# Inverse square roots of both layer norms: eleven operations on two engines, or one power operation on GpSimd

## The chip, the cores and the metric

The kernel runs on one core of a Trainium2 chip. The metric is the device time of one execution in microseconds (us), the median over runs of the same program. The core has a matrix engine (TensorE, PE in the profile, with PEld for its weight loads), a vector engine (VectorE, DVE), an activation engine (ScalarE, ACT), GpSimd (POOL) and a queue for transfers (SyncE, SP). [...]

## The reference, cut to what matters

Two layers of the same kind run one after the other on an image `x` of 512 x 512 positions with 64 channels, in float32. Both first normalise over groups of two channels of the whole image (`_gn`). Then, for each position:

```python
xn = _ln(x, norm_scale, norm_bias)                      # inner norm over 64 channels
left = (xn @ Wl + bl) * mask * sigmoid(xn @ Wlg + blg)  # 128 hidden channels
right = (xn @ Wr + br) * mask * sigmoid(xn @ Wrg + brg)
out_gate = sigmoid(xn @ Wog + bog)
out = _banded_ingoing(left, right, 4)     # 9 neighbouring rows, weighted by left
out = _ln(out, out_norm_scale, out_norm_bias) * out_gate   # outer norm over 128
return out @ Wo + bo                                    # added to x by the caller
```

and `_ln` is `(x - m) / sqrt(v + eps) * scale + bias`. So every position needs two inverse square roots, one for the inner norm and one for the outer norm, and every layer needs 32 more for its groups.

## The kernel before, in words

The rows are cut into 9 overlapping blocks of 64 and the columns into chunks of 128 positions per half. The work goes in steps: one step (a "unit") brings 8 columns of both halves into the machine, 128 partitions x 512 values, called `z`. There are 288 units per layer, and the stages of one unit are spread over some 30 steps, so that in one step each engine works on several units of different ages.

What an engine does in one step, and in which order, is written out by hand: the lists `FIRST` and `SECOND` (lines 36 to 55) name the stages for the first and the second layer. The loop at line 872 walks the list and emits each stage's instructions, and every engine keeps that program order (`InOrder`, line 383). Therefore nearly every row of the profile carries line 391. The groups have to be told apart by the tiles that they write and read.

GpSimd does most of the elementwise work on `z`: it scales (`z<-z,ga`) and moves it (`z<-z,gb`) for the group norm, centres it (`z<-z,sti`) and rescales it (`z<-z,rs`) for the inner norm, and adds a bias to the rows that come back in (`XR<-XR,fewer` or `both`). VectorE does the statistics (`sti`, `sto`), the product with the sigmoid (`RO<-banks,sg`), and the copies of the banded product back into `RO`.

In every fourth step `solve` (line 623) collects 32 inner and 32 outer variances of each partition into one tile `var` of 128 x 64 and takes their inverse roots into `rs`. The stages are these:

- "solve on a": ScalarE writes the inner half of `var` and the negated outer means `nm`.
- "solve on p": GpSimd writes the outer half of `var` in two operations.
- "solve on d": VectorE writes a first guess into `rs`, one operation on the bits of `var` taken as integers.
- "roots": GpSimd improves that guess in ten operations on 128 x 64 (`rsqrt`, lines 173 to 182), then multiplies the outer part by the mask and `nm` by the result. The items `("roots", 2)` and `("roots", 99)` emit two, or all remaining, of these.

`rs` and `nm` are then read by GpSimd (`z<-z,rs`, "rescale") and by ScalarE (`on<-RO,nm,rs`, "norm") in later steps. Between "solve on p" and "roots" GpSimd has one large operation on `z` in both lists; among the roots it has none.

The same function `rsqrt` serves `group_affine` (line 325), once per layer, ahead of its first unit; there all eleven operations are on VectorE, and their result `ga` is needed by the first `z<-z,ga`.

Of the kernel before, what the change touches and what calls it, by code (L numbers as in the profile page):

```python
# [8 lines left out]
F32 = mybir.dt.float32  # L9
I32 = mybir.dt.int32  # L10
AF = mybir.ActivationFunctionType
ALU = mybir.AluOpType
# [4 lines left out]
P = 128  # L17
# [11 lines left out]
NB = 32  # L29
# [8 lines left out]
    ("out stats", 3), ("project", 4), "turn", "centre", ("sigmoid", 0), "move",  # L38
    "scale next", ("out stats", 99), "solve", "bias", ("solve on", "p"), ("right", 0),
    "last product", "rescale", ("solve on", "a"), ("sigmoid", 4), ("norm", (0, 4)),  # L40
    ("solve on", "d"), "transpose", ("roots", 2), ("right", 4), ("band", 0), "keep",
    ("copy a", 0), ("band", 1), ("roots", 2), "sums", ("copy a", 1), ("roots", 2),
    "norm columns", ("roots", 2), ("roots", 99), "times gate", "move next", ("copy b", 0),
    ("copy b", 1), ("norm", (4, 8)), "end",
# [2 lines left out]
    ("out stats", 2), "gates", "centre", ("out stats", 3), ("project", 0), ("project", 4),  # L47
    ("sigmoid", 0), "scale", "rescale", "gated", ("out stats", 99), "inner stats",
    ("right", 0), "solve", "turn", "scale next", "last product", ("solve on", "p"),
    ("solve on", "a"), ("solve on", "d"), "transpose", ("sigmoid", 4), "move", ("roots", 2),  # L50
    "times gate", "end", ("roots", 2), ("band", 0), ("norm", (0, 4)), "norm columns",
    ("roots", 2), ("roots", 2), "keep", ("right", 4), ("copy a", 0), ("band", 1),
    ("roots", 99), ("norm", (4, 8)), ("copy b", 0), "move next", ("copy a", 1),
# [51 lines left out]
def tile_two_banded_layers(  # L105
# [6 lines left out]
    nc = tc.nc  # L112
# [7 lines left out]
    const = ctx.enter_context(tc.tile_pool(name="const", bufs=1))  # L120
    sm = ctx.enter_context(tc.tile_pool(name="sm", bufs=2))
# [30 lines left out]
        same.rearrange("p (g t) -> p g t", t=2), last(pair, 2), 1.0 / (2.0 * L * L), None, ALU.mult  # L152
    )

    def one_bank():
        return ps.tile([P, 512], F32, tag="ps", name="bank")

    def two_banks():
        return ps2.tile([P, 1024], F32, tag="ps2", name="banks")

    def rsqrt(o: bass.AP, v: bass.AP, vec=nc.vector, e=nc.vector) -> list:


        p, n = v.shape
        t, u = (
            sm.tile([P, 3 * NB], F32, tag=f"rsqrt{i}", name="rsqrt", bufs=1)[:p, :n]
            for i in range(2)
        )
        return [
            lambda: vec.tensor_scalar(  # L170
                o.bitcast(I32), v.bitcast(I32), -0.5, float(0x5F3759DF), ALU.mult, ALU.add
            ),
            lambda: e.tensor_tensor(t, o, o, ALU.mult),
            lambda: e.tensor_tensor(t, t, v, ALU.mult),
            lambda: e.tensor_scalar(u, t, -10.0 / 3.0, None, ALU.add),
            lambda: e.tensor_tensor(t, t, u, ALU.mult),
            lambda: e.tensor_scalar(t, t, 5.0, None, ALU.add),
            lambda: e.tensor_tensor(o, o, t, ALU.mult),
            lambda: e.tensor_tensor(t, o, o, ALU.mult),
            lambda: e.tensor_tensor(t, t, v, ALU.mult),  # L180
            lambda: e.tensor_scalar(t, t, -27.0 / 1024.0, 0.5625, ALU.mult, ALU.add),
            lambda: e.tensor_tensor(o, o, t, ALU.mult),
        ]

    PARTS = (
        ("right", 2 * H), ("left", 2 * H), ("gate", H), ("Wo", D), ("ob", 1),
# [60 lines left out]
    def solve_layer(i: int, f: dict, r: dict, tmp, half: bass.AP):  # L247
# [9 lines left out]
        for nm, lo, hi in (("right", 0, 2), ("left", 2, 4), ("gate", 4, 5)):  # L257
            lo, hi = lo * H, hi * H
            pm = one_bank()[:, : hi - lo]
            nc.tensor.matmul(pm, lhsT=half, rhs=aug[:, lo:hi], start=True, stop=True)  # L260
            pb = one_bank()[:, : hi - lo]
            nc.tensor.matmul(pb, lhsT=hb, rhs=raw[:, lo:hi], start=True, stop=False)
            nc.tensor.matmul(pb, lhsT=ones_row, rhs=brow[:, lo:hi], start=False, stop=True)
            nc.vector.tensor_tensor(r[nm], aug[:, lo:hi], pm, ALU.subtract)
            nc.vector.tensor_tensor(r[nm], r[nm], pb, ALU.add)
# [14 lines left out]
        nc.vector.tensor_scalar(r["Wo"], f["wo"], osc, None, ALU.mult)  # L280

        pb = one_bank()
        nc.tensor.matmul(pb[:, :D], lhsT=ones_row, rhs=f["bo"], start=True, stop=True)
        if i == 0:
# [40 lines left out]
    def group_affine(mean: bass.AP, var: bass.AP, pool):  # L325

        ve = pool.tile([P, D], F32, name="g_ve")
        nc.vector.tensor_scalar(ve, var, GN_EPS, None, ALU.add)
        for f in rsqrt(ga, ve):
            f()  # L330
        nc.vector.scalar_tensor_tensor(gb, mean, -1.0, ga, ALU.mult, ALU.mult)
# [291 lines left out]
    def solve(w: dict, ins: list, outs: list, sti, sto) -> dict:  # L623

        ni, no = len(ins) * JU, len(outs) * JU
        v = sm.tile([P, 3 * NB], F32, tag="var", name="var", bufs=1)[:, : ni + no]
        r = sm.tile([P, 3 * NB], F32, tag="rs", name="rs", bufs=3)[:, : ni + no]
        pairs = lambda x: x.rearrange("p (k t) -> p k t", t=2)
        act, pool = [], []
        if ni:  # L630
            of = sti[:, : ni // 2, 2::3]
            act.append(
                lambda: en.scalar.activation(
                    pairs(v[:, :ni]), of, AF.Identity, bias=ln_eps, scale=1.0 / D
                )
            )
            for n, u in enumerate(ins):
                u.rs = r[:, n * JU : (n + 1) * JU]
        if no:

            js = slice(outs[0].m, outs[0].m + no)
            vo = v[:, ni:]
            nm = sm.tile([P, NB], F32, tag="nm", name="nm")[:, :no]
            act.append(lambda: en.scalar.mul(pairs(nm), sto[:, :, 1::3], -1.0))
            pool += [
                lambda: en.gpsimd.tensor_tensor(
                    pairs(vo), sto[:, :, 2::3], pairs(w["m2"][:, js]), ALU.mult
                ),
                lambda: en.gpsimd.tensor_scalar(vo, vo, LN_EPS, None, ALU.add),
            ]  # L650
        seed, *todo = rsqrt(r, v, en.vector, en.gpsimd)
        if no:
            ro = r[:, ni:]
            todo.append(lambda: en.gpsimd.tensor_tensor(ro, ro, w["m"][:, js], ALU.mult))
            todo.append(lambda: en.gpsimd.tensor_tensor(nm, nm, ro, ALU.mult))
            for n, o in enumerate(outs):
                o.rs, o.nm = ro[:, n * JU : (n + 1) * JU], nm[:, n * JU : (n + 1) * JU]
        return {"a": act, "p": pool, "d": [seed], "roots": todo}

    def norm(o: Out, lo: int, hi: int, pool: bool):  # L660
        if lo == 0:
# [107 lines left out]
    def layer(src: bass.AP, dst: bass.AP, w: dict, stats: bool, then=None):  # L769
# [61 lines left out]
        for t in range(min(loads), last_t + 3):  # L831
# [40 lines left out]
            for item in order:  # L872
# [51 lines left out]
                elif name == "end" and p:  # L924
                    ended(dst, p)
                elif name == "sums" and t - 2 in outs:
                    sums(outs[t - 2], t - 2 == first_t, t - 2 == last_t)
                elif name == "solve" and t % 4 == 0:
                    st, us = sti.pop((t + 4) // 4, (None, []))
                    so, os = sto or (None, [])  # L930
                    sto = None
                    if us or os:
                        solving = solve(w, us, os, st, so)
                elif name == "solve on":
                    for f in solving.pop(n, []):
                        f()
                elif name == "roots" and solving:
                    for f in solving["roots"][:n]:
                        f()
                    del solving["roots"][:n]  # L940
                elif name == "norm" and t + 1 in outs:
                    lo, hi = n
                    norm(outs[t + 1], lo, min(hi, JU - nv), False)
                elif name == "norm columns" and t + 1 in outs:
                    norm(outs[t + 1], JU - nv, JU, True)
                elif name == "band" and len(mixing) > n:
                    c, h0 = mixing[n]
                    mixed.append(mix(c, A[c, h0 // HA], h0, stats))
                elif name == "copy a" and len(mixing) > n:
                    en.scalar.copy(*mixed[n][0])  # L950
                elif name == "copy b" and len(mixing) > n:
                    en.vector.tensor_copy(*mixed[n][1])
# [81 lines left out]
    keep = ctx.enter_context(tc.tile_pool(name="keep", bufs=1))  # L1034
# [39 lines left out]
def build(arrays):  # L1074
    import concourse.bacc as _bacc

    nc = _bacc.Bacc("TRN2", target_bir_lowering=False, num_devices=1)
    aps = {}
    for name in _INS:
        a = arrays[f"in_{name}_dram"]  # L1080
        aps[name] = nc.dram_tensor(
            f"in_{name}_dram", a.shape, mybir.dt.from_np(a.dtype), kind="ExternalInput"
        ).ap()
    out = nc.dram_tensor("out_0_dram", aps["x"].shape, F32, kind="ExternalOutput").ap()
    layers = [{n: aps[f"L{i}_conv_{n}"] for n in _NAMES} for i in range(2)]
    with tile.TileContext(nc) as tc:
        tile_two_banded_layers(tc, aps["x"], layers, out)
    return nc
# [10 lines left out]
```

## Time and profile before

| | |
|---|---|
| median of 3 runs | 4811.89 us (4810.83 to 4814.79) |
| the profiled execution's own time | 4837.72 us |
| its span | 4835.9 us |
| busy share of the span | PE 81%, ACT 78%, DVE 77%, POOL 73% |
| granted TensorE clock, mean | 0.942 |

The profiled execution is 25.8 us, or 0.5%, above the median of the runs; 1.8 us of its time lie outside its span. No engine is busy all the time: four of them share the load almost evenly, and the time is set by what they wait for from one another.

Both steady stretches are long: 500 to 2500 us lies within the first layer and 2900 to 4700 us within the second. At 230 and at 2628 us a layer starts, and before 230 us the image is read once for its statistics.

### The profile page before, as it was taken

To read this page: it belongs to the slowest core of one execution; us is meant where nothing else is said; L and a number is where in the kernel's file an instruction comes from. 1 tells how busy PE (TensorE), PEld (TensorE's weight loads), DVE (VectorE), ACT (ScalarE), POOL (GpSimd) and SP (SyncE) were. 2 spreads that over 40 slices of the span, in tenths; PEclk is the share of its full clock that TensorE was granted. 3 is DMA by queue.
4 is the path that set the end of the run, shared out by engine and by line. 5 is a ranking of instruction groups with operands and counts; after the bars stand their busy time and mean duration, and the time that the engine had idled before them with its cause. 6 is when DMAs were issued, how large, how long until landed. Compare 5 with 4: busy or idle time off the path is not lost.

```text
span 4835.9 us, 192971 instructions
## 1 busy us (share of the span) xinstructions
PE 3899.5 (81%) x76306; PEld 3340.4 (69%) x76306; DVE 3737.4 (77%) x9061; ACT 3749.9 (78%) x9022; POOL 3530.7 (73%) x4739
## 2 busy tenths in 40 slices
PE   1035899989998989998985479888888888888898
PEld 0034677777887877887864467777777777777775
DVE  7854777777777777777766468888888888888887
ACT  0023788888888888888886259989888898889899
POOL 0046888888888988998833588878877787777751
PEclk9987999999999999999998689999999999999999
DMA  7968677777777777777764768877777787778776
GB/s 314 393 112 123 175 202 202 203 204 204 199 205 203 208 199 201 207 207 202 199 182 131 72 164 221 223 214 218 216 217 217 211 221 213 218 215 220 218 205 178
DMA packets 1437807, 983.47 MB, mean 203 GB/s; under 512 B 167362, under 2 KB 1284584, under 8 KB 1432552
## 3 DMA queue, kind: packets, MB, share of 16 engines
q1 hardware_dynamic: 1432064, 969.69, 73.7%
q8 instruction: 604, 9.90, 0.9%
q14 instruction: 299, 2.45, 0.2%
q10 hardware_dynamic: 4840, 1.43, 0.1%
HBM read 658.35 MB, written 312.40 MB: 201 GB/s over the span
## 4 chain that ended last, share of the span: by engine, by line
PE 35%; ACT 16%; DMA 11%; POOL 11%; issue 9%; DVE 6%; SPq 4%; POOLq 0%; DVEq 0%; ACTq 0%
PE bank L391 17%; PE banks L391 16%; ACT on L391 9%; POOL z L391 7%; SPq L391 4%; DMA zg<-later 3%; DMA XR<-in_x_dram 3%; ACT gate L391 2%; PE acc L391 2%; ACT zT L391 2%; ACT sg L391 2%; DMA z<-mid_x 2%; POOL rsqrt L391 2%; DVE RO L391 1%; DVE sto L391 1%
## 5 line engine op out<-in xcount | busy, mean ns | idle before, releaser
L391 ACT ACTIVATE on<-RO,nm,rs 128x128 f32<-128x128 f32 x4608 | 1939.9, 509 | 24.5 <-PE bank L391 12.4
L391 PEld LDWEIGHTS banks<-pack,zT 64*128 64x128 f32 x18576 | 1288.9, 203 | 431.7 <-ACT zT L391 250.6
L391 PE MATMUL banks<-pack,zT 64*128 64x128 f32 x18576 | 1321.8, 291 | 213.7 <-ACT zT L391 175.7
L391 DVE TENSOR_TENSOR RO<-banks,sg 128x512 f32<-128x512 f32 (+1 forms) x1188 | 785.0, 674 | 488.5 <-ACT sg L391 367.4
L391 ACT ACTIVATE sg<-banks 128x512 f32<-128x512 f32 (+1 forms) x1188 | 693.3, 598 | 357.6 <-PE banks L391 348.9
L391 POOL TENSOR_TENSOR z<-z,ga 128x512 f32<-128x512 f32 x536 | 682.4, 1282 | 311.9 <-DMA z<-mid_x 214.3
L391 PE MATMUL bank<-zg,pack 64*128 64x448 f32 (+1 forms) x2304 | 684.9, 622 | 194.9 <-DMA zg<-later 123.0
L391 DVE SCALAR_TENSOR_TENSOR ZH<-bank,pack,gate 128x448 f32<-128x448 f32 (+1 forms) x1152 | 739.7, 683 | 95.2 <-ACT gate L391 76.8
L391 DVE BATCH_NORM_STATS2 sto<-RO 128x6 f32<-128x256 f32 x2304 | 799.0, 410 | 2.0 <-ACT RO L391 0.3
L391 POOL TENSOR_TENSOR z<-z,gb 128x512 f32<-128x512 f32 x536 | 681.9, 1281 | 5.0
L391 PE MATMUL bank<-pack,ZH 128*64 128x64 f32 x18432 | 665.7, 225 | 13.1 <-ACT gate L391 11.8
L391 POOL TENSOR_TENSOR z<-z,rs 128x512 f32<-128x512 f32 x586 | 621.2, 1061 | 16.5
L391 PEld LDWEIGHTS bank<-pack,ZH 128*64 128x64 f32 x18432 | 585.9, 138 | 57.3 <-ACT gate L391 22.0
L391 POOL TENSOR_TENSOR z<-z,sti 128x512 f32<-128x512 f32 x586 | 625.1, 1068 | 0.0
L391 ACT ACTIVATE gate<-bank 128x448 f32<-128x448 f32 (+1 forms) x1152 | 568.3, 550 | 49.5 <-PE bank L391 29.0
L391 DVE BATCH_NORM_STATS2 sti<-z 128x6 f32<-128x128 f32 x2344 | 501.7, 280 | 11.6 <-POOL z L391 5.9
L391 ACT ACTIVATE zT<-banks 128x512 f32<-128x512 f32 (+1 forms) x1084 | 470.2, 494 | 30.0 <-PE banks L391 23.5
L391 PE MATMUL bank<-ident,on 64*128 64x64 f32 x9216 | 450.4, 227 | 41.2 <-ACT gate L391 27.2
L391 PEld LDWEIGHTS bank<-ident,on 64*128 64x128 f32 x9216 | 415.4, 141 | 92.4 <-ACT gate L391 37.0
L391 PE MATMUL banks<-RO,A 64*64 64x128 f32 x9216 | 338.0, 289 | 105.9 <-DVE RO L391 99.2
L391 PEld LDWEIGHTS bank<-zg,pack 64*128 64x128 f32 x2304 | 221.6, 193 | 276.5 <-issue 67.3
L391 DVE TENSOR_TENSOR XR<-bank,XR 120x512 f32<-120x512 f32 (+1 forms) x576 | 391.2, 679 | 1.5 <-PE bank L391 0.8
(150 smaller groups left out, 4021.3 us busy)
## 6 DMA issues: line engine op xcount, KB each, us to landing
later<-zT SPq DMA_DIRECT2D x576, 256.0 KB
A<-left_of SPq DMA_DIRECT2D x1152, 128.0 KB
zg<-later SPq DMA_DIRECT2D x576, 256.0 KB
z<-in_x_dram SPq DMA_DIRECT2D x576, 128.0 KB
z<-mid_x SPq DMA_DIRECT2D x576, 128.0 KB
gn_x<-in_x_dram SPq DMA_DIRECT2D x16, 4096.0 KB
XR<-in_x_dram SPq DMA_DIRECT2D x448, 112.0 KB
mid_x<-XR SPq DMA_DIRECT2D x448, 112.0 KB
```

Source lines behind the costliest of these rows:

```text
L391: return lambda *a, **k: tc.keep_in_program_order(f(*a, **k))
```

## The change

`rsqrt` becomes one GpSimd operation, a tensor-tensor operation with the power operator, whose second operand is a column of -0.5 spread over the row. The two scratch tiles and the guess on VectorE go. "solve on d" leaves both lists; all other items keep their places. `group_affine` calls the same function, so its root goes to GpSimd as well.

```diff
-    ("solve on", "d"), "transpose", ("roots", 2), ("right", 4), ("band", 0), "keep",
+    "transpose", ("roots", 2), ("right", 4), ("band", 0), "keep",
...
-    ("solve on", "a"), ("solve on", "d"), "transpose", ("sigmoid", 4), "move", ("roots", 2),
+    ("solve on", "a"), "transpose", ("sigmoid", 4), "move", ("roots", 2),
...
+    minus_half = const.tile([P, 1], F32, name="minus_half")
+    nc.vector.memset(minus_half, -0.5)
...
-    def rsqrt(o: bass.AP, v: bass.AP, vec=nc.vector, e=nc.vector) -> list:
+    def rsqrt(o: bass.AP, v: bass.AP, e=nc.gpsimd) -> list:
         p, n = v.shape
-        t, u = (
-            sm.tile([P, 3 * NB], F32, tag=f"rsqrt{i}", name="rsqrt", bufs=1)[:p, :n]
-            for i in range(2)
-        )
-        return [
-            lambda: vec.tensor_scalar(
-                o.bitcast(I32), v.bitcast(I32), -0.5, float(0x5F3759DF), ALU.mult, ALU.add
-            ),
-            lambda: e.tensor_tensor(t, o, o, ALU.mult),
...
-            lambda: e.tensor_tensor(o, o, t, ALU.mult),
-        ]
+        return [lambda: e.tensor_tensor(o, v, minus_half[:p].broadcast_to([p, n]), ALU.pow)]
...
-        seed, *todo = rsqrt(r, v, en.vector, en.gpsimd)
+        todo = rsqrt(r, v, en.gpsimd)
...
-        return {"a": act, "p": pool, "d": [seed], "roots": todo}
+        return {"a": act, "p": pool, "roots": todo}
```

The order of instructions on TensorE, ScalarE and the SP queue is the same in both kernels. On VectorE the 160 guesses, the two chains of eleven in `group_affine` and nothing else are gone. On GpSimd each ten-operation chain is one operation in the same place, and two power operations for `group_affine` are added.

More of the change, by code (lines that the diff above doesn't have):

```diff
@@ L159, in two_banks @@
         return ps2.tile([P, 1024], F32, tag="ps2", name="banks")
-    def rsqrt(o: bass.AP, v: bass.AP, vec=nc.vector, e=nc.vector) -> list:
+    def rsqrt(o: bass.AP, v: bass.AP, e=nc.gpsimd) -> list:
         p, n = v.shape
-        t, u = (
-            sm.tile([P, 3 * NB], F32, tag=f"rsqrt{i}", name="rsqrt", bufs=1)[:p, :n]
-            for i in range(2)
-        )
-        return [
-            lambda: vec.tensor_scalar(
-                o.bitcast(I32), v.bitcast(I32), -0.5, float(0x5F3759DF), ALU.mult, ALU.add
-            ),
-            lambda: e.tensor_tensor(t, o, o, ALU.mult),
[L174 to L177, printed above, removed]
-            lambda: e.tensor_tensor(o, o, t, ALU.mult),
[L179 to L182, printed above, removed]
-        ]
+        return [lambda: e.tensor_tensor(o, v, minus_half[:p].broadcast_to([p, n]), ALU.pow)]
     PARTS = (
```

## The prediction

> **What bounds the kernel now.** I read the page's first part and its chain, then VectorE's and GpSimd's waits, then GpSimd's groups by shape, then one solve in the timeline, and at last the chain around a solve.
>
> ```profile
> PE 3899.5 (81%) x76306; PEld 3340.4 (69%) x76306; DVE 3737.4 (77%) x9061; ACT 3749.9 (78%) x9022; POOL 3530.7 (73%) x4739
> ...
> PE 35%; ACT 16%; DMA 11%; POOL 11%; issue 9%; DVE 6%; SPq 4%; POOLq 0%; DVEq 0%; ACTq 0%
> ```
>
> No engine is full, and the chain that ended last goes through all of them; POOL holds 11% of it, and `POOL rsqrt` is listed with 2%, some 97 us. The work that goes is thus partly on the path.
>
> ```profile
> DVE rs L391 <- POOL var L391: 161.4, 93, 4.8
> DVE rs L391 <- ACT var L391: 16.8, 38, 0.5
> POOL rsqrt L391 <- DVE rs L391: 65.0, 24, 28.9
> POOL z L391 <- DMA z<-mid_x: 214.3, 71, 7.3
> ```
>
> These are waits: total us, times, longest. VectorE stands still for 178 us in all because its first guess (`rs`) waits for `var`, mostly for GpSimd's half of it. GpSimd in turn waits 65 us for that guess, nearly all of it where a layer starts. GpSimd also has true slack: it waits for loads.
>
> ```profile
> L391 POOL TENSOR_SCALAR rsqrt<-rsqrt 128x64 f32<-128x64 f32 x384 | 125.3, 326 | 33.6
> L391 POOL TENSOR_TENSOR rsqrt<-rsqrt,var 128x64 f32<-128x64 f32 x256 | 81.9, 320 | 20.0
> L391 POOL TENSOR_TENSOR rsqrt<-rsqrt,var 128x32 f32<-128x32 f32 x44 | 11.1, 252 | 3.5
> ```
>
> Groups: busy us and mean ns of one, then idle before them. An operation of 64 columns takes 320 ns and one of 32 takes 252, so 68 ns for 32 columns, 2.1 ns a column, and 184 ns fixed; about 80 ns of idle follow each.
>
> ```profile
> 1020.93 0.23 POOL var L391
> 1021.16 0.08 issue
> 1021.24 0.30 POOL var L391
> 1021.54 0.02 issue
> 1021.56 0.04 DVE rs L391
> 1021.60 0.07 issue
> 1021.67 0.69 DVE RO L391
> 1022.37 0.04 issue
> 1022.41 1.60 PE banks L391 x47
> ```
>
> This is the chain (start, us): GpSimd's `var` releases the guess, behind it in VectorE's queue stands `RO`, and TensorE waits for `RO`. The guess itself is 0.2 us; the harm is that it ties VectorE's queue to GpSimd's position.
>
> **The change part by part.** *VectorE's guess goes.* 160 operations of 0.195 us are 31 us of VectorE, 77% busy; worth nothing by themselves. What counts is the wait. From 500 to 2500 us (67 solves of the first layer) the guess waits 126.5 us for GpSimd; from 2900 to 4700 us (64 solves of the second) 26.0 us for GpSimd and 16.3 for ScalarE. Followed back in stretches of 50 us, the chain goes through the guess in 40 of the 67 solves: 126.5 x 40/67 = 75 us. `RO` also needs ScalarE's `sg` (367 us of VectorE's waits), so I let half reach the end: 38 us, bounds 0 and 75. For the second layer 5 us. What is late next is `sg` or the banded product's copy to `RO`.
>
> *Ten GpSimd operations go.* In one solve they run from 1209.95 to 1213.93 us, start to next start: 3.98 us, some 640 us over 160 solves. Nothing else moves: the order on TensorE, ScalarE and SP is unchanged, and no DMA moves.
>
> *One power operation comes; call its time P, for 64 columns.* No row shows it, and it decides everything. From below: it cannot be under the 0.32 us of a plain multiply of that size. [...] I take 3.0: its nearest row is the root it replaces, ten operations whose column work is only 1.35 of 3.98 us, the rest being paid ten times where the power pays once. The ends kept are 1.2 and 14.
>
> [...]
>
> *What P does on the path.* At 3.0 us each solve frees 0.98 us of GpSimd, a quarter of the chain's root. `rsqrt` pieces with their issue gaps hold about 97 x 1.3 = 126 us of the chain; a quarter is 30 us.
>
> *Waits added.* Power waits for ScalarE's half of `var` directly; the guess waited at most 0.5 us for it, 38 times. Queued behind the power are the two small products and the next `z<-z,gb`. One operation on `z` (1.05 us in the first layer, 1.29 in the second) lies between GpSimd's own `var` and the power, which hides this wait: nothing, at most 17 us.
>
> *Starts of layers.* The first guess stands in VectorE's queue behind group-norm work: `var` is ready at 267.5 us and the guess starts at 277.84; in the second layer 2639.6 and 2645.19. The power needs neither: 10.3 + 5.6 us sooner, against which TensorE then waits for GpSimd's `z`. The two `group_affine` roots (2.73 us each on VectorE, from 2625.23 to 2627.96) become P and two handovers of about 0.1 us, 1 us worse together. I take a gain of 10 us.
>
> Sum: 38 + 5 + 30 + 10 = 83 us off the profiled execution's 4837.7 us; it lies 25.8 us above the median, and the saving is taken off that median: 4811.9 - 83, about 4730 us.
>
> **The rivals.** *GpSimd becomes the bound (slower).* In 500 to 2500 us a solve's cycle is 2000/67 = 29.85 us and GpSimd waits 198 us in all, 2.96 a cycle; without wait and without the root it needs 29.85 - 2.96 - 3.98 = 22.9. In 2900 to 4700 the cycle is 28.1, waits 319/64 = 5.0, the need 19.1. If half of the waits stay (loads still come late), the cycles are 24.4 + P and 21.6 + P. They pass the present cycle at P = 5.5 us in the first layer and 6.5 in the second. From there each further us costs 131 us. P = 8 gives 67 x 2.55 + 64 x 1.5 = 267 us, 5080 us; P = 14 gives 67 x 8.55 + 64 x 7.5 = 1053 us, 5865 us. For it: GpSimd's slack is that small, and a power is no simple operation. Against: the ten operations pay ten fixed parts.
>
> [...]
>
> *No change.* The gains of VectorE and GpSimd meet what is late next (`sg`, loads), or P lands near 5 us and eats them: 4812 us. TensorE is 90% busy in 500 to 2500 us (1809.8 of 2000), so there is little beyond it to gain.
>
> **How the numbers follow.** A run of this kernel can be told from no change at about 0.2%, 10 us. The forecast (P under 5.5 us, a net gain): 0.45. No change: 0.04. GpSimd the bound, P from 5.5 to 14 us: 0.34; dearer still: 0.17. So faster 0.45, same 0.04, slower 0.51: the single likeliest case is a gain, though the slower ones together weigh a little more, since the range of P is open upwards only. The forecast's own range is 4650 (P about 1.2 us: 2.8 x 160 us less on GpSimd, a quarter of it on the path, 110 us, with the other gains 53) to 4800; the whole range goes up to 5865, where P = 14, and leaves out 0.17 above and a little below.
>
> **What would show it.** Right: a group `rs<-var,minus_half` 128x64 on POOL at about 3 us; no VectorE wait for `POOL var`; POOL busy near 3531 - 495 (the ten-operation groups' sum) + 160 x 3 = 3516 us; PE's share up. The step on the stall is wrong if VectorE's `RO` then waits as much longer for `sg`. The forecast is wrong if that group is over 5.5 us: then POOL is the busiest engine, its waits for loads shrink, and TensorE, VectorE and ScalarE wait for `POOL z`, `rs` and `nm`.

## The result, and the profile after

The changed kernel takes 5477.82 us (median of 4 runs, 5469.13 to 5479.72); the kernel before took 4811.36 us beside it. The ratio is 1.1387, with a 95% interval of 1.1363 to 1.1412: slower by 13.9%. The forecast was 4730 us, a gain; the time lies within the whole range, in the case that had GpSimd as the bound. Ratios here and below leave out the one execution, of 13315 us among six of one experiment, that ran in a slow state.

The page of the changed kernel: busy time by engine, then two of its groups.

```profile
PE 4061.1 (74%) x76306; PEld 3457.5 (63%) x76306; DVE 3700.6 (68%) x8880; ACT 3760.4 (69%) x9022; POOL 4593.6 (84%) x3301
...
L376 ACT ACTIVATE on<-RO,nm,rs 128x128 f32<-128x128 f32 x4608 | 1926.7, 500 | 843.9 <-POOL nm L376 809.4
...
L376 POOL TENSOR_TENSOR rs<-var,minus_half 128x64 f32<-128x64 f32 (+4 forms) x160 | 1541.2, 9632 | 32.5 <-ACT var L376 29.3
```

GpSimd has 1438 instructions less and is busy 1063 us more. It is now the busiest engine, and the busy share of all others has fallen. ScalarE's `on`, which waited 10.7 us for `nm` before, now waits 809 us for it. The chain of waits on this page covers only the last moments of the run, so it is not shown; windows and waits take its place.

GpSimd's groups with shapes kept apart (busy us, mean ns of one, idle before):

```profile
L376 POOL TENSOR_TENSOR rs<-var,minus_half 128x64 f32<-128x64 f32 x128 | 1351.0, 10554 | 1.3 <-ACT nm L376 1.3
L376 POOL TENSOR_TENSOR rs<-var,minus_half 128x32 f32<-128x32 f32 x22 | 119.8, 5447 | 5.1 <-ACT var L376 3.9
...
L168 POOL TENSOR_TENSOR ga<-on,minus_half 128x64 f32<-128x64 f32 x1 | 10.5, 10534 | 8.9 <-DVE on L313 8.9
```

This is the price that no row of before had. 64 columns cost 10.55 us and 32 cost 5.45, so a column costs 160 ns and the fixed part 0.34 us; a plain multiply costs 2.1 ns a column (320 ns for 64 columns and 252 for 32 in the kernel before).

One solve in the timeline of the changed kernel (start, us, engine; in brackets the wait before):

```profile
1217.86 10.55 POOL L376 TENSOR_TENSOR rs<-var,minus_half 128x64 f32<-128x64 f32 x1
...
1228.49 0.24 POOL L376 TENSOR_TENSOR rs<-rs,pack 128x32 f32<-128x32 f32 x1
1228.81 0.25 POOL L376 TENSOR_TENSOR nm<-nm,rs 128x32 f32<-128x32 f32 x1
1229.02 1.27 POOL L376 TENSOR_TENSOR z<-z,gb 128x512 f32<-128x512 f32 x1
1229.10 1.66 ACT L376 ACTIVATE on<-RO,nm,rs 128x128 f32<-128x128 f32 x4 [8.11 <-POOL nm L376]
...
1230.32 0.88 DVE L376 BATCH_NORM_STATS2 sti<-z 128x6 f32<-128x128 f32 x4 [6.71 <-POOL z L376]
1230.66 0.84 ACT L376 ACTIVATE zT<-banks 128x512 f32<-128x512 f32 x2
...
1231.29 2.93 PE L376 MATMUL banks<-pack,zT 64*128 64x128 f32 x24 [7.20 <-ACT zT L376]
```

The power runs from 1217.86 to 1228.41 us, and GpSimd's next operation starts at 1228.49. ScalarE stands 8.1 us for `nm`, and `zT`, which needs nothing of the root, stands behind `on` in its queue; TensorE waits 7.2 us for that `zT`. VectorE waits 6.7 us for a `z` that GpSimd had not yet moved for the group norm (`z<-z,gb`). One long operation stops three engines. The waits of the whole run (total us, times, longest) say the same; first three of the kernel before, then the changed kernel's:

```profile
PEld banks L391 <- ACT zT L391: 270.3, 221, 17.5
ACT on L391 <- POOL nm L391: 10.7, 15, 1.1
DVE sti L391 <- POOL z L391: 5.9, 6, 1.7
```

```profile
PEld banks L376 <- ACT zT L376: 970.5, 332, 16.6
ACT on L376 <- POOL nm L376: 809.4, 143, 10.4
...
DVE sti L376 <- POOL z L376: 281.3, 76, 10.2
...
POOL z L376 <- DMA z<-mid_x: 90.0, 28, 5.7
```

GpSimd's wait for the loads of `mid_x` fell from 214 to 90 us, and from 500 to 2500 us it is busy 1929 of 2000 us, where it was busy 1729: its slack is all but spent.

### The profile page after: what moved, and what is told of

Read it like the earlier page. It is cut to its first block, busy times and chain, and to the rows that moved or that the text cites. A ratio compares the mean times of both kernels' runs of the same rounds, so it can differ in the third digit from the quotient of the medians.

```text
span 5474.8 us, 191257 instructions
## 1 busy us (share of the span) xinstructions
PE 4061.1 (74%) x76306; PEld 3457.5 (63%) x76306; DVE 3700.6 (68%) x8880; ACT 3760.4 (69%) x9022; POOL 4593.6 (84%) x3301
## 5 line engine op out<-in xcount | busy, mean ns | idle before, releaser
L376 PEld LDWEIGHTS banks<-pack,zT 64*128 64x128 f32 x18576 | 1355.4, 218 | 953.5 <-ACT zT L376 788.7
L376 PE MATMUL banks<-pack,zT 64*128 64x128 f32 x18576 | 1427.2, 309 | 675.7 <-ACT zT L376 629.8
L376 POOL TENSOR_TENSOR rs<-var,minus_half 128x64 f32<-128x64 f32 (+4 forms) x160 | 1541.2, 9632 | 32.5 <-ACT var L376 29.3
L376 PE MATMUL bank<-zg,pack 64*128 64x448 f32 (+1 forms) x2304 | 656.4, 615 | 128.7 <-ACT RO L376 115.6
L376 PE MATMUL bank<-pack,ZH 128*64 128x64 f32 x18432 | 706.6, 233 | 10.6 <-ACT gate L376 10.0
L376 PEld LDWEIGHTS bank<-pack,ZH 128*64 128x64 f32 x18432 | 626.4, 146 | 56.9 <-ACT gate L376 15.7
L376 DVE COPY RO<-banks 128x512 f32<-128x512 f32 x288 | 199.1, 692 | 530.0 <-ACT RO L376 530.0
L376 PE MATMUL bank<-ident,on 64*128 64x64 f32 x9216 | 465.0, 238 | 53.8 <-ACT gate L376 31.1
L376 PEld LDWEIGHTS bank<-ident,on 64*128 64x128 f32 x9216 | 432.9, 153 | 109.7 <-ACT gate L376 42.1
```

Of the source, the lines that this page charges most:

```text
L376: return lambda *a, **k: tc.keep_in_program_order(f(*a, **k))
```

## The experiments

The kernel before took 4838 to 4842 us beside these runs, which were made on three chips, so ratios are used. "Length" is the time from the start of the root to the start of the product with the mask, for 64 columns: 3.98 us before and 10.63 in the changed kernel. "First layer" is the time from one `gb` of VectorE to the next in the profiled execution: 2402 us before, 2744 in the changed kernel. The second group norm's root lies in it: 2.73 us before, 10.5 where it is a power.

### A multiply in the place of the power

```diff
-        todo = rsqrt(r, v, en.gpsimd)
+        todo = [lambda: en.gpsimd.tensor_tensor(
+            r, v, minus_half.broadcast_to(list(v.shape)), ALU.mult)]
```

> The root itself is left out: a plain multiply of 128 x 64 by -0.5 stands where the power stood (the two roots of the group norm stay powers), so P is some 0.32 us instead of 10.55 and all else is the changed kernel. Theory A (all of the loss is the power's length on GpSimd): the cycles of 24.4 + P and 21.6 + P us no longer bind and the prediction's other terms can be seen by themselves: 38 + 5 + 10 us from VectorE's freed queue and the layer starts, and with 3.58 us less on GpSimd per solve (a quarter of 573 us on the path) some 140 more: about 4620 us, 4580 to 4760. Rival B (the chain moved by the lost first guess is worth nothing, since sg or loads end last there): 4770 to 4812. Rival C (the loss has another cause than the power's length): still above 5000.

Measured: 4728.25 us, ratio 0.9773 (0.9759 to 0.9788). The cause is the power in the solves, and rival C falls; whether it is the power's length, the padding below tells. The gain is 110 us where theory A's sum had about 190: a root that costs next to nothing, with VectorE free of it, brings 2.3%.

### The power on half of the columns

```diff
+            lambda: en.gpsimd.tensor_tensor(r[:, :half_n], v[:, :half_n], mh, ALU.pow),
+            lambda: en.gpsimd.tensor_tensor(r[:, half_n:], v[:, half_n:], mh, ALU.mult),
```

> The power runs on the first half of the columns only (the inner variances in a usual solve), the second half takes a plain multiply in its place, which leaves the outer roots out. P is then 5.45 us (the row of 128 x 32) + 0.25 us + one gap, 5.8 us, just about the point at which the prediction's formula sees no change. Theory A (throughput of GpSimd): 24.4 + 5.8 = 30.2 against 29.85 us in the first layer, 27.4 against 28.1 in the second, 67 x 0.35 = +23 us, less up to 50 us for VectorE's queue: 4780 to 4850. Rival D (what counts is how late rs and nm are, with 1.8 us more than before against 6.6 in the changed kernel): a quarter of the 666 us, about 4980.

Measured: 4899.01 us, ratio 1.0125 (1.0108 to 1.0143), between the two theories. With the multiply, this and the changed kernel, there are three lengths: 0.37 us gives 0.9773, 5.87 gives 1.0125, 10.63 gives 1.1387. The mean slope is 0.64% per us (31 us) up to 5.87, and (1.1387 - 1.0125)/4.76 = 2.65% per us (128 us) beyond. The latter agrees with the rival's 131 us for each further us; where its corner lies is taken up below.

### The same load without a power, ahead of the products or behind them

```diff
+        pad = sm.tile([P, 3 * NB], F32, tag="pad", name="pad", bufs=1)[:, : ni + no]
+        padding = round(6 + 0.31 * (ni + no)) * [
+            lambda: en.gpsimd.tensor_tensor(pad, v, v, ALU.mult)]
...
-    "transpose", ("roots", 2), ("right", 4), ("band", 0), "keep",
+    "transpose", ("roots", 99), ("right", 4), ("band", 0), "keep",
...
+        todo += padding                      # first run: ahead of the products
-        return {"a": act, "p": pool, "roots": todo}
+        return {"a": act, "p": pool, "roots": todo + padding}    # second run: behind
```

The second layer's list has the same edit; by it all of a solve's operations are emitted in one place. The root itself is a plain multiply here.

> The power's twin without the power: a plain multiply in its place (the root is left out) and 26 multiplies of 128 x 64 into a scratch tile behind it, ahead of the two small products; at 0.40 us from start to start that is some 10.4 us (fewer for smaller solves). Theory A: time as of the changed kernel, 5478 within 60 us, since only the length on GpSimd counts. Rival C (the power hurts in another way than by its length, for example by holding what VectorE shares with GpSimd): clearly under 5400 us, with VectorE's and ScalarE's operations shorter than in the changed kernel.

> As the run before, with the 26 scratch multiplies behind the two small products instead of ahead of them: GpSimd carries the same load, but rs and nm are ready early. Theory A in its pure form (throughput: GpSimd's work on z is late whatever stands first): as the run before, within 60 us of 5478. Rival D (lateness of rs and nm, which holds ScalarE's queue and with it TensorE): far less, 4650 to 5000 us, and ScalarE's wait for nm (809 us in the changed kernel) gone.

Measured: ahead 5369.03 us, ratio 1.1101 (1.1082 to 1.1119); behind 5189.02 us, ratio 1.0722 (1.0706 to 1.0738). Ahead, the time is below theory A's band and on rival C's side of 5400 us. Most of that gap is length: the padding came out at 9.76 us in place of 10.63; 0.87 us at 2.65% are 2.3%, so a ratio of 1.116 was due and 1.110 came. Some 0.6%, with 0.3% either way by the two intervals, is left for anything in a power other than its length. Rival C's other sign is missing: VectorE's and ScalarE's operations are as long as in the changed kernel (`on` 500 ns in both, `RO` 675 here and 676 there, `sto` 411 in both). Behind, the time lies between the two theories. The waits of the two runs, ahead first:

```profile
PEld banks L376 <- ACT zT L376: 904.3, 329, 20.1
PE banks L376 <- ACT zT L376: 730.1, 262, 20.0
ACT on L376 <- POOL nm L376: 693.1, 141, 9.5
```

```profile
DVE sti L376 <- POOL z L376: 560.2, 238, 8.1
PEld banks L376 <- POOL z L376: 557.8, 190, 7.2
```

With the products ready early, `on` hardly stands for `nm` (35 us in place of 693), and the work on `z` is late instead. Neither theory holds alone. Of the 13.3% between the multiply (0.9773) and the padding ahead (1.1101), 3.8% go with the lateness of `rs` and `nm`, and 9.5% stay when they are early: GpSimd's time itself.

### The tie of VectorE to GpSimd, alone and with a short root

The first run moves the guess to GpSimd, the second keeps one VectorE operation in the guess's place but makes the root a multiply.

```diff
-        seed, *todo = rsqrt(r, v, en.vector, en.gpsimd)
+        todo = rsqrt(r, v, en.gpsimd, en.gpsimd)             # first run: guess on GpSimd
...
-        seed, *todo = rsqrt(r, v, en.vector, en.gpsimd)
+        seed = lambda: en.vector.tensor_scalar(r, v, -0.5, 1.0, ALU.mult, ALU.add)
+        todo = [lambda: en.gpsimd.tensor_tensor(r, r, v, ALU.mult)]   # second run: tie and multiply
```

> The kernel before with its first guess on GpSimd instead of VectorE, as the first of then eleven operations; nothing else moves. It does that part of the change that frees VectorE's queue, and leaves the length of the root as it was, plus one operation (some 0.4 us from start to start). The runs with a multiply and with half a power lie at 0.9773 and 1.0125 for lengths of 0.37 and 5.87 us, 0.65% per us, so 0.4 us are +0.2 to 0.3%. Theory A (the prediction's term: VectorE's 178 us of waits for the guess are worth 43 us, 0.9%): ratio 0.992 to 0.996. Rival B (RO then waits for sg or the loads, the waits are worth nothing): 1.001 to 1.004.

> One VectorE operation on var stays in the place of the first guess, and one GpSimd multiply in the place of the ten operations; the root itself is left out, the group norm's roots stay on VectorE. Beside the run with the multiply alone (0.9773) it tells what VectorE's tie to GpSimd costs when the root is short. Theory A: the tie costs 43 us, 0.9%, so 0.984 to 0.988 (the group norm's two powers, 2 x 8 us, stand against it: 0.981 to 0.985). Rival B (the tie is worth nothing): 0.972 to 0.977.

Measured: guess on GpSimd 4826.70 us, ratio 0.9964 (0.9951 to 0.9978), just above theory A's range. Tie and multiply 4815.47 us, ratio 0.9949 (0.9925 to 0.9974), above what both had. The wait that the first guess causes is still there in the second run:

```profile
DVE rs L391 <- POOL var L391: 157.2, 93, 4.6
```

So cutting the tie alone gives 0.4% (with a root 0.35 us longer), cutting the root to almost nothing with the tie kept gives 0.5%, and both together give 2.3%. The first layer shows it plainly: 2402 us before, 2381 with the tie cut, 2394 with the root cut, 2297 with both. The gains do not add. In the first run other waits stand in the tie's place: `on` waits 124.4 us for `nm` (10.7 before), `sti` 47.7 us for `z` (5.9 before), and `RO` 427.1 us for `sg` (367.4 before), the prediction's own sign that part of the stall only moves. With both cut, `on` does not wait for `nm` at all, and `sti` waits 2.7 us. Why `nm` comes late once the tie is gone was not followed.

### The outer half of `var` on VectorE

```diff
-                lambda: en.gpsimd.tensor_tensor(
+                lambda: en.vector.tensor_tensor(
                     pairs(vo), sto[:, :, 2::3], pairs(w["m2"][:, js]), ALU.mult
                 ),
-                lambda: en.gpsimd.tensor_scalar(vo, vo, LN_EPS, None, ALU.add),
+                lambda: en.vector.tensor_scalar(vo, vo, LN_EPS, None, ALU.add),
```

> The kernel before with the two operations that write the outer half of var on VectorE instead of GpSimd, just ahead of the first guess. VectorE then waits for ScalarE's half alone and has some 0.45 us more to do per solve; GpSimd has 0.72 us less (1208.22 to 1208.94 in the timeline of the kernel before). Theory A: 0.9% for the waits and 0.65% x 0.72 = 0.5% for GpSimd, less what 0.45 us cost on VectorE: 0.986 to 0.993. Rival B (the waits are worth nothing): 0.995 to 1.000, since only GpSimd's 0.72 us count.

Measured: 4812.24 us, ratio 0.9939 (0.9927 to 0.9952): faster than before, and between the two theories. In the first layer only:

> The outer half of var on VectorE in the first layer only, the second layer as before; all at full precision. In the run with var on VectorE in both layers the profiled first layer was 29 us shorter (2373.0 against 2401.9 us from gb to gb), the second about 12 longer. If that harm in the second layer is real: 0.991 to 0.994, below the 0.9939 of both layers. If not (scatter of single profiles): 0.994 to 0.997.

Measured: 4817.26 us, ratio 0.9939 (0.9918 to 0.9961). The same as with both layers, so the second layer's 12 us are not confirmed. With the guess of the first layer on GpSimd besides:

> First layer: outer half of var on VectorE and the guess on GpSimd, so that VectorE waits for nothing of a solve and GpSimd's share is 0.3 us shorter than before; second layer as before; full precision. Theory F: the tie is cut (about 0.6% by the run with the guess on GpSimd, 0.9964 with 0.4 us more on GpSimd), 0.3 us less is 0.2% more, and VectorE's two operations cost what they took in the run with var on VectorE, some 0.58 us each: 0.989 to 0.994. Rival (VectorE's two operations, taking three times their time beside GpSimd's, eat it): 0.995 to 1.000.

Measured: 4817.41 us, ratio 0.9946 (0.9926 to 0.9966), between its two ranges. At full precision no version came below 0.9939.

### The whole solve of the first layer on VectorE

`solve` takes VectorE for every GpSimd operation in the first layer.

> The kernel before with the whole solve of the first layer on VectorE (both var operations, guess, ten improvements, mask and nm: fifteen operations at 0.2 to 0.26 us, some 3.3 us), the second layer as it was. GpSimd loses 5.2 us per solve in the first layer, where it waits least. If GpSimd's length is what counts (theory A): the first layer gains what the run with the multiply gained there and pays 3.3 us on VectorE instead of the 1.9 us that it stood waiting, ratio 0.985 to 0.998. Rival E (VectorE's queue is as tight as GpSimd's, and every us ahead of RO holds TensorE): 1.005 to 1.03.

Measured: 5192.80 us, ratio 1.0720 (1.0705 to 1.0735), far outside both. The first layer takes 2744 us, as long as in the changed kernel. In the timeline (VectorE's and GpSimd's lines):

```profile
1209.49 0.23 DVE L391 TENSOR_TENSOR rsqrt<-rs 128x64 f32<-128x64 f32 x1
...
1211.20 1.14 DVE L391 TENSOR_TENSOR rsqrt<-rsqrt 128x64 f32<-128x64 f32 x1
1212.21 1.04 POOL L391 TENSOR_TENSOR z<-z,rs 128x512 f32<-128x512 f32 x1
1212.37 0.93 DVE L391 TENSOR_SCALAR rsqrt<-rsqrt 128x64 f32<-128x64 f32 x1
...
1215.44 1.18 POOL L391 TENSOR_TENSOR XR<-XR,fewer 120x512 f32<-120x512 f32 x1
1215.60 1.10 DVE L391 TENSOR_TENSOR rsqrt<-rsqrt,var 128x64 f32<-128x64 f32 x1
1216.73 0.19 DVE L391 TENSOR_SCALAR rsqrt<-rsqrt 128x64 f32<-128x64 f32 x1
1216.96 0.23 DVE L391 TENSOR_TENSOR rs<-rs,rsqrt 128x64 f32<-128x64 f32 x1
...
1217.33 1.04 POOL L391 TENSOR_TENSOR z<-z,rs 128x512 f32<-128x512 f32 x1 [0.71 <-DVE rs L391]
1217.44 0.97 DVE L391 TENSOR_TENSOR nm<-nm,rs 128x32 f32<-128x32 f32 x1
```

VectorE's operations of 0.2 us take about 1 us, the length of GpSimd's large operations beside them; the solve's fifteen operations take 8.6 us here, where some 3.3 were expected. In the 0.71 us in which GpSimd stands idle (up to 1217.33) they take 0.19 and 0.23. TensorE's next `bank<-zg,pack` came after a wait of 7.65 us for `ZH`, which stands behind the solve.

### A shorter root, free of VectorE

Guess and six operations; the four that refine it to 1.5e-7 are left out and the constants are fitted, so the roots are exact to 2.5e-5. In the first run `first` is true in both layers, in the second in the first layer only.

```diff
+        a, b = -10.0 / 3.0, (5.0, None, ALU.add)
+        if e is not nc.vector:
+            a, b = -3.334408576881946, (4.997394119779261, 0.3755184465129126, ALU.add, ALU.mult)
...
-            lambda: e.tensor_scalar(u, t, -10.0 / 3.0, None, ALU.add),
+            lambda: e.tensor_scalar(u, t, a, None, ALU.add),
...
-            lambda: e.tensor_scalar(t, t, 5.0, None, ALU.add),
+            lambda: e.tensor_scalar(t, t, *b),
...
-        seed, *todo = rsqrt(r, v, en.vector, en.gpsimd)
+        seed, *todo = rsqrt(r, v, en.gpsimd if first else en.vector, en.gpsimd)
+        todo = todo[:6]
```

> The root of both norms wholly on GpSimd as a guess and six operations: the last four, which refine a relative error of about 2.5e-5 to 1.5e-7, are left out (constants fitted for that), so it computes the roots less exactly; the group norm's roots stay as before. GpSimd's root is 7 operations, some 2.9 us, and VectorE is free of it. Theory F (both loads end at the same place: cutting VectorE's tie or the root's length alone gives 0.4 to 0.5%, both together 2.3%, so with the tie cut each us off the root counts): on the line between the run with the guess on GpSimd (0.9964 at 4.4 us) and the run with the multiply (0.9773 at 0.37 us, less 16 us for its two long group powers, so 0.974): 0.986 to 0.990. Rival (the line is not straight, only a root of almost nothing gives the gain): 0.993 to 0.997.

> The short root of seven operations (roots less exact, as in the run with the short root on GpSimd), with the guess on GpSimd in the first layer and on VectorE in the second. The second layer's tie costs little (26 + 16 us of waits in the kernel before), and GpSimd saves 0.4 us per solve there. Theory F with the tie placed in the first layer: equal to the run with the guess on GpSimd in both, or better by up to 0.3%: 0.984 to 0.990. If the tie matters in the second layer too: worse by 0.2 to 0.5%.

Measured: 4755.74 us, ratio 0.9812 (0.9786 to 0.9837), at a length of 2.70 us (1209.01 to 1211.71 us); and 4764.34 us, ratio 0.9844 (0.9820 to 0.9868), with the second layer's guess on VectorE. The first is below theory F's numbers; whether the tie costs anything in the second layer stays open, since the two intervals overlap. Both beat both kernels, at the price of that precision. With the tie cut, the length thus counts with real roots too: 1.63 us less than in the run with the guess on GpSimd bring 1.5%.

## Why the prediction was wrong

**The step that failed is the price of the power: "I take 3.0".** It measured 10.55 us, 3.5 times that. No run shows the 3.0, nor the ends of 1.2 and 14 us: all three were the author's guesses. In their place the runs showed 160 ns a column, 76 times the 2.1 ns of a multiply, and a fixed part of 0.34 us. The argument that the power pays the fixed part once while ten operations pay it ten times was true, and too small: nine fixed parts of 0.26 us (184 ns and some 80 of idle, in the kernel before) are 2.3 us. Between ends as far apart as 1.2 and 14 us, the point was set by an argument on structure, not by a row, and the sign of the forecast hung on it alone.

**The rival's formula came close, partly by luck.** It had cycles of 24.4 + P and 21.6 + P us. With P = 10.55 that is 34.95 and 32.15 us. The changed kernel has 57 solves from 500 to 2500 us, 35.1 us each, and 62 from 3200 to 5200, 32.3 us each. Its 67 x 5.1 + 64 x 4.05 = 601 us count the solves of two windows; the whole profiled executions differ by 638.9 us (the medians by 666): 341.7 in the first layer, 289.4 in the second, 7.8 ahead of them. The 7.8 are the first group norm's power (10.54 us in place of 2.73); the second's lie in the 341.7, and both together had been priced at 1 us.

The luck lies in the mechanism. The formula counts GpSimd's time alone. At the padding's 9.76 us it gives 67 x 4.31 = 289 us in the first layer and 64 x 3.26 = 209 in the second. The padding behind the products, which is GpSimd's time alone, cost 221 and 117 us there; the padding ahead of them, which also makes `nm` late and so holds ScalarE's queue, cost 282 and 232 (each against the kernel before, with 7.8 us of group norm taken off the first layer). So for GpSimd's time alone the formula says too much (part of the difference may be what VectorE's freed queue gains), and the lateness that it leaves out about makes up for it.

**Where the corner lies.** By the runs without a tie, 1.0 is crossed at a length between 4.33 us (0.9964) and 5.87 (1.0125). In the first layer the formula holds at 5.87: 30.27 us a solve, and 2000/66 = 30.30 were measured. In the second it has no loss below 6.5 us, yet that layer took 22 us longer than before; there the corner is too late.

**The gains are not a sum.** "38 us, bounds 0 and 75" for VectorE's queue and "a quarter" for GpSimd's freed time were added. With a short root, cutting the tie took the first layer from 2394 to 2297 us, 97 us with the group norm's long power against it, above the upper bound; with the long root it was 21 us (2402 to 2381), within the bounds. With the tie kept, 3.6 us less on GpSimd for each of 160 solves gave 25 us (0.51% of 4842), 4% of 576 and not a quarter. The sum for P = 3.0, 83 us or 1.7%, is close to the 1.9% of the short root at 2.70 us, but its terms did not hold one by one: VectorE's was too small, GpSimd's too large as long as the other wait stood.

**What came as said:** VectorE's wait for `POOL var` is gone; GpSimd is the busiest engine and its waits for loads shrank, the signs named for a price above 5.5 us; in the changed kernel the first root starts at 264.86 us and ends at 269, where the guess had started at 277.84; the order on the other engines is the same. The gains among these do not outweigh 6.6 us on GpSimd in each solve.

## What to carry to other kernels

Fewer instructions were no measure here: before one operation takes the place of ten, run it once alone, since 64 columns cost 0.3 us in a multiply and 10.6 in a power. Where the price is unknown, work out the price at which the engine's idle time is used up, and forecast from how much of the possible range lies beyond it. Two waits that run beside each other are tested apart and together: here each alone brought half a per cent and both 2.3%.

## What the runs showed of the hardware that was not expected

In the changed kernel a GpSimd tensor-tensor operation with the power operator takes 10.55 us for 64 columns of 128 partitions and 5.45 for 32, the same in both layers (10.549 to 10.557 us over 57 operations from 500 to 2500 us, a median of 10.555 from 3200 to 5200). By these two sizes that is 160 ns a column and 0.34 us fixed. That line gives 4.2 us for 24 columns, 6.7 for 40 and 8.0 for 48; those powers, all of them near the start or the end of a layer, took 4.17 and 5.37, 6.74 to 6.86, and 8.06 to 8.58.

In the run with the whole solve of the first layer on VectorE, its short operations are stretched beside GpSimd's large ones. In the solve shown, those that start while GpSimd is at a `z` or `XR` operation take 0.67 to 1.22 us, the others 0.18 to 0.23, so that the solve moved to VectorE cost 8.6 us of its queue there, where 3.3 were worked out. It is so for an operation with two input tiles (1.22 us at 1213.34) and for one with a single one (0.93 us at 1212.37). The product `RO<-banks,sg`, which reads TensorE's product, was not stretched in the same stretch of time: 0.69 us at 1208.66, where GpSimd stood idle, and 0.68 at 1209.89, beside its `z<-z,ga`. In the run with the outer half of `var` on VectorE in both layers, the two `var` operations averaged 0.61 and 0.58 us where the shortest took 0.17 and 0.18. No run shows why some operations are stretched and others not.

The powers of the changed kernel do not stretch VectorE's operations in this way, long as they are. At the starts of the layers VectorE does some of the `z<-z,ga` and `z<-z,gb` itself, 128 x 512 with two inputs. In the changed kernel 22 of these ran wholly within a power and took 0.67 to 0.75 us; beside GpSimd's `z` operations they took up to 1.55 us (two took 2.98 us from 292.81 on, against 0.69 us for one at 287.85, within the power that runs from 282.52 to 291.04). This fits the padding: what a power costs is nearly all its length on GpSimd.
